# First attention of a two-layer decoder: the reciprocal root of the head norms moved from Newton steps on VectorE to one power on GpSimd

## Chip, cores and metric

The kernel runs on one core of one Trainium2 chip. The metric is the device time of one execution in microseconds (us). The engines are TensorE (PE; its weight loads are listed apart as PEld), VectorE (DVE), ScalarE (ACT), GpSimd (POOL) and SyncE (SP, which issues most of the transfers). Each engine takes its instructions strictly in order.

## What is computed

A decoder of two layers on x of 4 sequences of 256 tokens with 256 features, and a context of 4 x 256 tokens with 128 features. Each layer adds an attention, a state-space block (a scan over time with 16 states for each of 256 channels) and a feed-forward block to x. The change is in the first attention alone, whose queries, keys and values are normalised head by head:

```python
def _layernorm_unit(x, eps=1e-06):
    mu = jnp.mean(x, axis=-1, keepdims=True)
    xc = x - mu
    var = jnp.mean(xc * xc, axis=-1, keepdims=True)
    return xc * jax.lax.rsqrt(var + eps)
# 8 query heads, 2 key heads and 2 value heads of width 32; q and k are rotated (RoPE) first
q = _layernorm_unit(q) * 256.0
k = _layernorm_unit(k)
v = _layernorm_unit(v)
scores = einsum('bhqd,bhkd->bhqk', q, k) / sqrt(32) + mask   # causal, window of 64
scores = tanh(scores / 30.0) * 30.0
out = softmax(scores) @ v
```

## The kernel before

The first attention goes sequence by sequence (b = 0 to 3, 256 tokens each, in two chunks of 128 partitions). `head0(b)` (L347 to L408) makes the layer norm of x, transposes it, multiplies by the joint weight of q, k and v (L356), rotates q and k (L366, L372, L373), and subtracts the mean of each head (L380, L381). For both chunks together there are 24 heads (2 x 12), so one tile `rs` of 128 x 24 holds the mean squares: ScalarE squares (L385), VectorE sums (L388) and adds the epsilon (L389). `rsqrt_steps` (L100 to L112) then makes the reciprocal root on VectorE in 13 small instructions: a first guess from the bits of the number (L104) and three Newton steps of four instructions each (L108 to L111), one after the other on the same two tiles. VectorE scales the queries into `qn` (L396) and the values into `vn` (L399) by it, GpSimd the keys into `krep` (L403, twice). `tail0(b)` (L419 to L514) transposes `qn` and `krep` (L424, L429), forms the scores on TensorE (L449, L453), takes tanh and exp on ScalarE (L462, L470), weights the values (L476 to L487), divides by the sums (`divide`, L412 and L413), transposes (L497), projects (L506) and adds to x (L514).

Between these, in the same stage, runs the scan of the first state-space block, which doesn't depend on x: 64 states in all (2 halves of the batch x 2 halves of the channels x 16). One state takes an exponential on ScalarE (L215), a product `db` on GpSimd (L217), the scan on VectorE (L218), a product `hc` on VectorE (L220), and a sum of `hc` into y, in turns by a TensorE product with the identity (L235) and by an addition on GpSimd (L237). The row tiles `bt` and `ct` come by DMA from SP's queue (L209); `db`, `hc`, `bt` and `ct` have three buffers each, and the scanned tile `h` two. `mamba_front` (L150 to L200) prepares a half of the batch, with two softplus activations (L190). Behind the stage come the gate of the state-space block (L252 to L271), the first feed-forward (L606 to L638), and the second layer (from L641), in which `rsqrt` (L662 to L667) already takes a power on GpSimd (L666), as `ln_stats` does for the layer norms (L126).

The order in which the instructions of one engine stand is not that of the text: when the program is built, a list scheduler merges the two streams of work by its own estimate of when each instruction can start. A change of one line therefore moves its neighbours too. ScalarE loads a table before an activation of another kind than the last (the exponential of L215 and the softplus of L190 are such kinds), so the number of table loads depends on the order.

The constant tile `nhalf` (L94, L95) is 128 x 24 and holds -0.5.

Of the kernel before, what the change touches and what calls it, by code (L numbers as in the profile page):

```python
# [14 lines left out]
ALU = mybir.AluOpType  # L15
# [26 lines left out]
def decoder_kernel(  # L42
# [27 lines left out]
    nc = tc.nc  # L70
# [6 lines left out]
    def ps(pool):  # L77
        return pool.tile([P, 512], F32, tag="ps", name="ps")
# [15 lines left out]
    nhalf = cpool.tile([P, 24], F32, name="nhalf")  # L94
# [5 lines left out]
    def rsqrt_steps(v, n):  # L100

        r_ = small.tile([P, n], F32, tag=f"rs_r{n}", name="rs_r")
        t_ = small.tile([P, n], F32, tag=f"rs_t{n}", name="rs_t")
        nc.vector.tensor_scalar(  # L104
            r_.bitcast(I32), v.bitcast(I32), -0.5, float(0x5F3759DF), ALU.mult, ALU.add
        )
        for _ in range(3):
            nc.vector.tensor_mul(t_, r_, r_)  # L108
            nc.vector.tensor_mul(t_, t_, v)
            nc.vector.tensor_scalar(t_, t_, -0.5, 1.5, ALU.mult, ALU.add)  # L110
            nc.vector.tensor_mul(r_, r_, t_)  # L111
        return r_  # L112
# [17 lines left out]
    def ln_transposed(b, dst, pool):  # L130

        nb, rs = ln_stats([x[:, 2 * b + c, :] for c in range(2)])
        pt = ps(pool)
        for c in range(2):
            xn = work.tile([P, HID], F32, tag="xn", name="xn")
            nc.scalar.activation(
                xn, x[:, 2 * b + c, :], AF.Identity, bias=nb[:, c : c + 1], scale=rs[:, c : c + 1]
            )
            for f in range(2):
                nc.tensor.transpose(  # L140
                    pt[:, f * 256 + c * P : f * 256 + (c + 1) * P], xn[:, f * P : (f + 1) * P], ident
                )
        nc.scalar.copy(dst, pt.rearrange("p (f t) -> p f t", f=2))
# [175 lines left out]
    with ExitStack() as ph:  # L319
# [27 lines left out]
        def head0(b):  # L347
            xnT = work.tile([P, 2, S], F32, tag="xnT", name="xnT")
            ln_transposed(b, xnT, pa)

            r = ap.tile([P, 2, 12, 32], F32, tag="r", name="r")
            rr = ap.tile([P, 2, 10, 32], F32, tag="rr", name="rr")
            for c in range(2):
                pq = ps(pa)
                for f in range(2):
                    mm(  # L356
                        pq[:, 0:384],
                        lhsT=xnT[:, f, c * P : (c + 1) * P],
                        rhs=wqkv0[:, f, :],
                        start=(f == 0),  # L360
                        stop=(f == 1),
                    )
                cos = cst[:, C_COS0 + 32 * c : C_COS0 + 32 * c + 32]
                sin = cst[:, C_SIN0 + 32 * c : C_SIN0 + 32 * c + 32]
                q3 = pq[:, 0:320].rearrange("p (h d) -> p h d", d=32)
                nc.vector.tensor_mul(  # L366
                    rr[:, c].rearrange("p h (two d) -> p h two d", two=2),
                    pq[:, 0:320].rearrange("p (h two d) -> p h two d", two=2, d=16)[:, :, ::-1, :],
                    sin.rearrange("p (two d) -> p two d", two=2).unsqueeze(1).to_broadcast([P, 10, 2, 16]),
                )  # L370

                nc.vector.tensor_mul(q3, q3, cos.unsqueeze(1).to_broadcast([P, 10, 32]))  # L372
                nc.vector.tensor_add(r[:, c, 0:10, :], q3, rr[:, c])  # L373
                nc.scalar.copy(
                    r[:, c, 10:12, :], pq[:, 320:384].rearrange("p (h d) -> p h d", d=32)
                )

            rf = r.rearrange("p c h d -> p (c h) d")
            mean = small.tile([P, 24], F32, tag="a0_mean", name="a0_mean")
            nc.vector.tensor_reduce(mean, rf, AX.X, ALU.add)  # L380
            nc.vector.scalar_tensor_tensor(  # L381
                rf, mean.unsqueeze(2).to_broadcast([P, 24, 32]), -1.0 / 32, rf, ALU.mult, ALU.add
            )
            sq = ap.tile([P, 24, 32], F32, tag="sq", name="sq")
            nc.scalar.activation(sq, rf, AF.Square)  # L385
            rs = small.tile([P, 2, 12], F32, tag="a0_rs", name="a0_rs")
            rs24 = rs.rearrange("p c h -> p (c h)")
            nc.vector.tensor_reduce(rs24, sq, AX.X, ALU.add)  # L388
            nc.vector.tensor_scalar(rs24, rs24, 1.0 / 32, 1e-6, ALU.mult, ALU.add)  # L389
            rs = rsqrt_steps(rs24, 24).rearrange("p (c h) -> p c h", c=2)  # L390
            qn = ap.tile([P, 2, 8, 32], F32, tag="qn", name="qn")
            krep = ap.tile([P, 2, 2, 4, 32], F32, tag="krep", name="krep")

            vn = ap.tile([P, 2, 2, 33], F32, tag="vn", name="vn")
            nc.gpsimd.memset(vn[:, :, :, 32:33], 1.0)
            nc.vector.tensor_mul(  # L396
                qn, r[:, :, 0:8, :], rs[:, :, 0:8].unsqueeze(3).to_broadcast([P, 2, 8, 32])
            )
            nc.vector.tensor_mul(  # L399
                vn[:, :, :, 0:32], r[:, :, 10:12, :], rs[:, :, 10:12].unsqueeze(3).to_broadcast([P, 2, 2, 32])  # L400
            )
            for c in range(2):
                nc.gpsimd.tensor_mul(  # L403
                    krep[:, c],
                    r[:, c, 8:10, :].unsqueeze(2).to_broadcast([P, 2, 4, 32]),
                    rs[:, c, 8:10].unsqueeze(2).unsqueeze(3).to_broadcast([P, 2, 4, 32]),
                )
            return qn, krep, vn  # L408
# [117 lines left out]

        s0 = []
        parts = [head0(0), head0(1)]
        for b in range(B):
            states(2)  # L530
            if b + 2 < B:
                parts.append(head0(b + 2))
            tail0(b, *parts[b], states)
            if b == 0:
                first.append(mamba_scan(mamba_front(0, 1, pf), psd, psy))
            if b == 0:

                with tc.issue_after(loads[-1]):
                    nc.sync.dma_start(out=wqkv1, in_=wqkv1_in)
# [647 lines left out]
```

## Time and profile before

| what | value |
|---|---|
| three timed runs | 898.4, 910.52 and 914.03 us, median 910.52 us |
| the profiled execution's own time | 899.79 us |
| its span, first to last instruction | 898.0 us (1.79 us lie around it) |
| mean granted TensorE clock | 0.947 of full speed |
| PE, DVE, ACT, POOL busy | 806.3, 588.0, 474.5, 423.5 us |
| first attention, first `qn` to last addition to x | 33.1 to 188.5 us of the span |
| last state of the first scan | ends at 251.4 us |

The times in the prediction are positions in the profiled execution's span. A line of a group reads: source line, engine, operation, tile written <- tiles read, shapes, count, then the busy time of all in us and the mean of one in ns, then the idle time of the engine just before them and what ended most of it. A line of a timeline reads: start and length in us, engine, line, operation, tiles, shapes. In the table by stretches each engine has its busy time and, in brackets, its number of instructions, and then comes the granted clock of TensorE.

### The profile page before, as it was taken

Reading aid. Unit: us, or ns where it says so; the run is one execution under the profiler, and the core shown is the slowest. Engines: PE = TensorE matmul, PEld = TensorE weight load, DVE = VectorE, ACT = ScalarE, POOL = GpSimd, SP = SyncE. Lnnn points to the kernel's source line nnn. Section 1 sums busy time; section 2 is a strip of 40 time slices with the busy share of each in tenths; the row PEclk is TensorE's granted clock in tenths of the full one; section 3 lists DMA queues with packets and bytes.
Section 4 is the critical chain, followed back from the end, with each engine's and each line's share of the span. In section 5 each row is a group of like instructions: output and inputs, shape, how many; then the busy total and the mean of one; then the engine's idle time right before and its main releaser. Section 6 shows DMA issues by size and latency. Waiting matters only on the chain.

```text
span 898.0 us, 10284 instructions
## 1 busy us (share of the span) xinstructions
PE 806.3 (90%) x3074; PEld 501.4 (56%) x3074; DVE 588.0 (65%) x1106; ACT 474.5 (53%) x1182; POOL 423.5 (47%) x427
## 2 busy tenths in 40 slices
PE   4888999978989887889788978997999999999997
PEld 1445656523444444647555755665666656666665
DVE  4799988985855588797769686787057676212121
ACT  2767544587949556657857754776333433211111
POOL 5456676976645527766547471422257751000000
PEclk9999767978998999999899989997999999999999
DMA  5347564583512401101112010000147753445442
GB/s 162 117 133 252 174 187 157 186 275 100 198 64 68 143 1 36 59 33 39 36 36 72 23 47 1 24 3 24 27 152 226 231 152 104 148 149 162 156 144 82
DMA packets 60999, 98.36 MB, mean 110 GB/s; under 512 B 6336, under 2 KB 26704, under 8 KB 60688
## 3 DMA queue, kind: packets, MB, share of 16 engines
q1 hardware_dynamic: 59232, 95.77, 33.6%
q10 hardware_dynamic: 1712, 1.94, 0.7%
q8 instruction: 24, 0.39, 0.2%
q14 instruction: 31, 0.25, 0.1%
HBM read 96.24 MB, written 1.44 MB: 109 GB/s over the span
## 4 chain that ended last, share of the span: by engine, by line
PE 51%; DVE 20%; ACT 10%; issue 5%; POOL 4%; DMA 1%; DVEq 0%; POOLq 0%; SPq 0%; ACTq 0%
PE ps L974 13%; PE ps L988 12%; PE ps L842 5%; DVE h L218 4%; PE ps L673 3%; DVE hc L220 2%; PE ps L606 2%; PE ps L630 2%; PE ps L827 2%; DVE ps L700 2%; ACT sc L799 2%; DVE qs L693 2%; PE ps L780 1%; ACT L215 1%; PE ps L235 1%
## 5 line engine op out<-in xcount | busy, mean ns | idle before, releaser
L217 POOL TENSOR_TENSOR db<-bt,du 128x512 f32<-128x512 f32 x128 | 162.4, 1280 | 90.7 <-DVE h L218 76.3
L218 DVE TENSOR_TENSOR_SCAN h<-h,db 128x512 f32<-128x512 f32 x128 | 152.9, 1217 | 25.9 <-ACT h L215 25.7
L974 PE MATMUL ps<-moe_xnT,w 128*128 128x512 f32 x272 | 129.0, 597 | 0.0
L988 PE MATMUL ps<-w,hT 128*128 128x256 f32 x544 | 128.7, 380 | 0.0
L979 DVE SCALAR_TENSOR_TENSOR hT<-ps,gr 128x512 f32<-128x512 f32 x64 | 44.1, 689 | 127.0 <-PE ps L974 127.0
L988 PEld LDWEIGHTS ps<-w,hT 128*128 128x128 f32 x544 | 103.2, 191 | 40.2 <-issue 29.4
L215 ACT ACTIVATE h<-dt,negA 128x512 f32<-128x512 f32 x128 | 86.2, 689 | 56.3 <-DVE hc L220 55.7
L980 ACT ACTIVATE hT<-hT 128x512 f32<-128x512 f32 x68 | 42.8, 629 | 133.8 <-DVE hT L979 133.6
L673 PE MATMUL ps<-wqkv,xnT 128*128 128x512 f32 x192 | 93.2, 597 | 8.0 <-DVE rq L665 5.6
L220 DVE TENSOR_TENSOR hc<-h,ct 128x512 f32<-128x512 f32 x128 | 85.1, 680 | 4.0 <-DMA ct<-bc 2.5
L227 POOL TENSOR_TENSOR y<-y,hc 128x512 f32<-128x512 f32 x64 | 80.8, 1274 | 7.1 <-DVE hc L220 7.1
L666 POOL TENSOR_TENSOR rq<-rq,nhalf 128x8 f32<-128x8 f32 x20 | 33.0, 1648 | 88.2 <-DVE rq L665 88.0
L974 PEld LDWEIGHTS ps<-moe_xnT,w 128*128 128x128 f32 x272 | 51.7, 191 | 36.5 <-issue 33.2
L688 ACT ACTIVATE sq<-ps 128x128 f32<-128x128 f32 x160 | 42.4, 282 | 46.2 <-PE ps L673 46.2
L799 ACT ACTIVATE sc<-sc,nm 128x256 f32<-128x256 f32 (+1 forms) x128 | 56.7, 449 | 12.2 <-DVE nm L794 8.0
L804 POOL TENSOR_TENSOR sc<-sc,rsum 128x512 f32<-128x512 f32 (+1 forms) x32 | 46.3, 1468 | 35.2 <-DVE rsum L802 33.6
L842 PE MATMUL ps<-wo,oT 128*128 128x256 f32 x256 | 57.0, 381 | 0.4 <-ACT oT L835 0.4
L842 PEld LDWEIGHTS ps<-wo,oT 128*128 128x128 f32 x256 | 48.1, 190 | 9.2 <-ACT oT L835 2.6
L673 PEld LDWEIGHTS ps<-wqkv,xnT 128*128 128x128 f32 x192 | 32.9, 190 | 29.1 <-issue 17.9
L235 PE MATMUL ps<-hc,ident 128*128 128x512 f32 x64 | 40.6, 723 | 8.1 <-DVE hc L220 8.1
L707 PE MATMUL ps<-ident,qr 128*128 128x128 f32 x160 | 28.7, 297 | 19.2 <-DVE qr L701 17.3
L237 POOL TENSOR_TENSOR y<-y,hc 128x512 f32<-128x512 f32 x32 | 40.8, 1275 | 10.4 <-DVE hc L220 5.3
(201 smaller groups left out, 1447.3 us busy)
## 6 DMA issues: line engine op xcount, KB each, us to landing
bt<-bc SPq DMA_DIRECT2D x96, 256.0 KB, 3.6
ct<-bc SPq DMA_DIRECT2D x96, 256.0 KB, 3.7
w<-in_w_dram SPq DMA_DIRECT2D x64, 256.0 KB, 3.4
gr<-gt SPq DMA_DIRECT2D x64, 256.0 KB, 3.5
wqkv<-in_wqkv_dram SPq DMA_DIRECT2D x1, 3072.0 KB, 14.4
wo<-in_wo_dram SPq DMA_DIRECT2D x1, 2048.0 KB, 8.9
x<-in_x_dram SPq DMA_DIRECT2D x4, 256.0 KB, 5.6
w<-in_ws_dram SPq DMA_DIRECT2D x4, 256.0 KB, 3.4
```

Source lines behind the costliest of these rows:

```text
L215: nc.scalar.activation(h, dt[:, c, :], AF.Exp, scale=negA[:, a : a + 1])
L217: nc.gpsimd.tensor_mul(db, bt, du[:, c, :])
L218: nc.vector.tensor_tensor_scan(h, h, db, 0.0, ALU.mult, ALU.add)
L220: nc.vector.tensor_mul(hc, h, ct)
L227: nc.gpsimd.tensor_add(y[:, c, :], y[:, c, :], state(n, c, bt, ct))
L235: mm(yp, lhsT=ident, rhs=hc, start=(n == 0), stop=(n == 14))
L673: mm(pq, lhsT=xnT[:, f, c * P : (c + 1) * P], rhs=wqkv1[:, f, ch * 512 : (ch + 1) * 512], start=(f == 0), stop=(f == 1),)
L799: nc.scalar.activation(part, part, AF.Exp, bias=nm[:, qc, j : j + 1], accum_out=rsum[:, qc, j : j + 1])
L804: nc.gpsimd.tensor_mul(part, part, rsum[:, qc, :].unsqueeze(2).to_broadcast([P, 4, w]))
L842: mm(pout[:, c * 256 : (c + 1) * 256], lhsT=oTs[h // 4][:, h % 4, c * P : (c + 1) * P], rhs=wo1[:, 8 * gp + h, :], start=(h == 0), stop=(h ...
L974: mm(ph_, lhsT=w[:, f * P : (f + 1) * P], rhs=xnT[:, f, :], start=(f == 0), stop=(f == 1))
L988: mm(po[t // 2][:, (t % 2) * 256 : (t % 2 + 1) * 256], lhsT=h[:, t * P : (t + 1) * P], rhs=w[:, 256:512], start=start and t % 2 == 0, stop ...
```

## The change

One line of `head0` is replaced. The 13 VectorE instructions of `rsqrt_steps` are gone from it, and one GpSimd instruction takes the 128 x 24 tile to the power -0.5 in place; `qn`, `vn` and `krep` then read this tile. `rsqrt_steps` itself stays, since the second feed-forward uses it on another tile (L945).

```diff
             rs24 = rs.rearrange("p c h -> p (c h)")
             nc.vector.tensor_reduce(rs24, sq, AX.X, ALU.add)
             nc.vector.tensor_scalar(rs24, rs24, 1.0 / 32, 1e-6, ALU.mult, ALU.add)
-            rs = rsqrt_steps(rs24, 24).rearrange("p (c h) -> p c h", c=2)
+            nc.gpsimd.tensor_tensor(rs24, rs24, nhalf, ALU.pow)
             qn = ap.tile([P, 2, 8, 32], F32, tag="qn", name="qn")
```

In the program built from it, DVE has 52 instructions fewer and POOL 4 more. The order of all engines is the same up to the first `head0`, differs in the first attention and the first feed-forward, and is the same again from the last addition of the first scan (L239 of its second half) to the end. ACT has three more table loads in the part that differs: two for the softplus of L190 and one for the exponential of L215.

## The prediction

> **What bounds the kernel now.** I read the table by stretches first, to see which engine is full where the change sits, then the groups of the removed lines in 28 to 126 us, then VectorE's timeline around one of the removed blocks, and last the groups of the powers that GpSimd takes already. The stretches (length, busy time of PE, PEld, DVE, ACT, POOL, granted clock, DMA):
>
> ```profile
> 48.00:63.00 15.00, 13.48 (x66) 7.98 (x64) 14.99 (x31) 8.51 (x16) 8.82 (x8) 0.89 0.54 168
> 63.00:81.00 18.00, 16.27 (x76) 10.13 (x75) 17.79 (x33) 12.55 (x24) 11.44 (x12) 0.91 0.47 119
> ...
> 107.00:126.00 19.00, 16.81 (x78) 10.54 (x76) 17.72 (x33) 10.07 (x23) 15.61 (x15) 0.77 0.52 158
> 126.00:188.00 62.00, 59.46 (x266) 37.92 (x266) 51.18 (x71) 33.08 (x65) 50.02 (x45) 0.85 0.58 183
> ```
>
> DVE has no idle time from 48 to 81 us (14.99 of 15, 17.79 of 18): there it sets the pace, and three of the four blocks of Newton steps lie in stretches of this kind. From 126 us on PE is full (59.46 of 62) at a granted clock of 0.85, and DVE has some 11 us to spare. POOL goes from 59% to 82%. So a microsecond of DVE is worth something up to about 126 us and little behind.
>
> ```profile
> L110 DVE TENSOR_SCALAR rs_t<-rs_t 128x24 f32<-128x24 f32 x12 | 5.4, 448 | 0.1
> L108 DVE TENSOR_TENSOR rs_t<-rs_r 128x24 f32<-128x24 f32 x12 | 5.4, 447 | 0.2
> ...
> L111 DVE TENSOR_TENSOR rs_r<-rs_r,rs_t 128x24 f32<-128x24 f32 x12 | 3.4, 282 | 0.2
> ...
> L104 DVE TENSOR_SCALAR rs_r<-a_rs 128x24 int32<-128x24 int32 x4 | 3.3, 819 | 0.0
> ...
> L109 DVE TENSOR_TENSOR rs_t<-rs_t,a_rs 128x24 f32<-128x24 f32 x12 | 2.1, 173 | 0.1
> ```
>
> The same 128x24 work takes 173 ns in one line and 819 ns in another: the steps are stretched. The timeline of the second block shows where:
>
> ```profile
> 48.74 0.68 DVE L220 TENSOR_TENSOR hc<-h,ct 128x512 f32<-128x512 f32 x1
> 49.34 0.78 DVE L104 TENSOR_SCALAR rs_r<-a_rs 128x24 int32<-128x24 int32 x1
> 50.04 0.48 DVE L366 TENSOR_TENSOR rr<-ps,cst 128x320 f32<-128x320 f32 x1
> 50.44 0.17 DVE L108 TENSOR_TENSOR rs_t<-rs_r 128x24 f32<-128x24 f32 x1
> ...
> 52.14 1.00 DVE L110 TENSOR_SCALAR rs_t<-rs_t 128x24 f32<-128x24 f32 x1
> ...
> 62.81 0.92 DVE L396 TENSOR_TENSOR qn<-r,rs_r 128x512 f32<-128x512 f32 x1
> ```
>
> L104 lasts 0.78 us and ends when a POOL addition (48.82 to 50.09) ends; L110 lasts 1.00 and ends with a POOL product (51.83 to 53.10). And the block isn't one piece: scans and rotations stand between its steps, so DVE is never idle in it.
>
> ```profile
> L666 POOL TENSOR_TENSOR rq<-rq,nhalf 128x8 f32<-128x8 f32 x20 | 33.0, 1648 | 88.2 <-DVE rq L665 88.0
> ...
> L126 POOL TENSOR_TENSOR ln_rs<-ln_rs,nhalf 128x2 f32<-128x2 f32 x24 | 17.0, 713 | 1.7
> ```
>
> A power on POOL grows with the elements per partition: 6 more of them cost 1648 - 713 = 935 ns, 156 ns each.
>
> **What goes.** I count what each block takes of DVE: from its first step to `qn`, less the spacing of the other instructions in it. Block 0: 30.27 (end of L389) to 33.12, nothing between, 2.85 us. Block 1: 49.34 to 62.81 is 13.47, less 6 rotation steps at 0.40, 3 scans at 1.13, 3 `hc` at 0.60 and a reciprocal at 0.12 (7.73), leaves 5.74. Block 2: 70.70 to 80.09 is 9.39, less 3 scans, 2 `hc`, a reciprocal and a division (5.06), leaves 4.33. Block 3: 107.51 to 123.88 is 16.37, less 6 scans, 5 `hc`, three small ones and an idle 1.28 (11.63), leaves 4.74. Sum 17.66 us of DVE.
>
> **What comes.** The power on 24 elements isn't in the trace. From the two rows, a fixed 0.40 and 24 x 0.156 make 4.14 us; in proportion to the nearer row, 3 x 1.648 makes 4.94, and it can't take less than the 1.65 of a third of its size. I take 4.14, since two rows lie on it, and keep 4.94 for the range. Handing over costs little: L665 ends at 316.04, the power of L666 runs from 316.12 to 317.76, and DVE goes on at 317.80, 0.12 in all. Behind the power, in the order built from the change, `qn` stands on DVE directly after L389 (block 0), after L389 and one `hc` (blocks 1 and 2) or after L389 and one scan (block 3). So DVE, which takes its queue in order, stands idle, and the rotations and scans that used to fill the block are queued behind `qn`. On POOL the power has an addition of y (L237) ahead of it in blocks 1 and 2, which needs the `hc` just made, and a `db` in block 3. The wait on DVE:
> - Block 0: 4.14 + 0.12 = 4.26. Against 2.85: +1.41.
> - Blocks 1 and 2, on the old clock of block 1: `hc` is over at 49.34, L237 at 50.09, the power at 54.26, `qn` at 54.30: 4.96 idle. Against 5.74 and 4.33: -0.78 and +0.63.
> - Block 3: the `db` runs beside the scan, 4.26. Against 4.74: -0.48.
>
> Sum 18.44 of waiting for 17.66 of steps: +0.78 us. POOL gains 4 x 4.14 = 16.6 us, but while DVE waits no scan frees a `db` buffer either, and up to three finished `db` stand ready when the wait ends, so I cost the delay of the next `db` (power and two `krep`, 1.7 us) at nothing; if that stock is gone, it costs up to 1.7 per head.
>
> **Earlier `qn`.** After L389, `qn` came 14.0, 9.6 and 16.4 us later in blocks 1 to 3; now about 5. That looks like a gain, but TensorE transposed these `qn` at 74.2, 108.1 and 140.7, against `qn` finished at 63.7, 80.9 and 125.2: it wasn't waiting. I cost it at nothing. SP issues the same row loads in a new order; the three waits of `hc` for `ct` there make 2.5 us in all, and I leave them as they are.
>
> **New order elsewhere.** Three more table loads on ACT at 1.28 us. Two split the two softplus at 85 to 90 us by an exponential; ACT waited 1.73 us for TensorE between these (L190 at 89.11), so 2 x 1.28 - 1.73 leaves +0.8. The third lies near 196 us, where ACT waited 1.17 and 2.60, and is hidden. There the new order also has a gain: the addition of the gate of sequence 1 (L271 at 206.59) no longer stands behind the second `du` (L193 at 203.66, after 3.29 idle). Its ceiling is these 3.29 us, its floor nothing; I take half, -1.6.
>
> Sum: 0.78 + 0.8 - 1.6 = 0.0 us. On the profiled execution's own time that is 899.8. This execution lies 10.7 below the median; the four readings of the old kernel are two pairs, 898.4 and 899.8, and 910.5 and 914.0, so a median may fall in either, and I predict their mean, 905.7, rounded to 906.
>
> **Rules weighed.** The stretched steps first: the rows show 0.17 us alone and 0.78 to 1.00 against a POOL instruction. The Trainium skill ("SBUF — State Buffer", Who interferes with whom) says that VectorE and GpSimd share a port pair as an exclusive lock, which a two-input VectorE instruction or a two-port mode asks for, so the later one waits to the end; the trace agrees with its 1.00 beside 1.27. It would speak against a 4 us power on POOL, which would hold that pair; here DVE has nothing else to do in that time, so the sum is the same by it. The price second: the rows give 156 ns per element. The skill ("GPSIMD Engine Reference", Performance versus the Vector engine) gives about 2.6 cycles per element for a two-input add at 1.2 GHz; an estimate from that page would be 0.05 us for 24 elements above the fixed part, and the sum some 15 us faster. No row of a power agrees with it.
>
> **The rivals.**
> - *GpSimd becomes the bound (slower).* For it: POOL is 82% busy in 107 to 126. Against it: three `db` buffers, and PE is the fuller engine behind 126. Price: 4 x 0.80 for the power at its upper end, 4 x 1.27 for one more POOL instruction ahead of it, 4 x 1.7 for `krep` ahead of the next `db`, 3.0 for uncovered table loads: 3.2 + 5.1 + 6.8 + 3.0 = 18 us, 2.0%, 929 from the median and 930 from the upper pair. It decides as soon as the `db` stock is empty when the power ends, in more than two heads. Chance 0.17.
> - *The waits are filled (faster).* If TensorE and ScalarE, which go on while DVE waits, remove later waits of DVE (4.1 us for L506, 2.7 for L356, 12.9 for L215 in 28 to 260), half of the 17.66 comes through: -9, 897 from the mean. Against it: the later half is TensorE's. Chance 0.16; with the readings' lower pair it ends at 890. The whole 17.66 would be the ceiling, 1.9%.
> - *The clock.* TensorE had 0.77 to 0.87 of its clock from 107 to 253 us with 132 us of work; 0.05 more or less there is 132 x 0.05 / 0.85 = 7.8 us, in either direction: 898 or 914. Chance 0.12.
> - *No change that can be told*, as forecast: 0.55, on its own within 896 to 917 by the readings' scatter.
>
> **How the numbers follow.** The range runs from the lower pair less 9 (890) to the upper pair plus 12, two thirds of the slow rival (924). Within 2%, about what a measurement of this kernel can tell from no change, is 892 to 929 about the median 910.5. The forecast, the clock, half of the fast rival (0.08) and a quarter of the slow one (0.04) stay inside: 0.55 + 0.12 + 0.08 + 0.04, rounded to 0.78. Slower 0.13, faster 0.09.
>
> **What would show it.** The power at about 4.1 us, and DVE idle 4.3 to 5.0 before each `qn`, released by POOL; idle time of DVE in 28 to 126 up from 7 to about 25 us, its busy time down by about as much; the last addition to x (187.8) within 3 us. Wrong would be: a power far from 4.1; scans waiting for `db` after `krep`; that addition more than 8 us away.

## The result, and the profile after

The changed kernel took 913.7 us (median of 20 executions, 904.98 to 919.2), the kernel before 905.16 us beside it (20 executions, 898.4 to 915.4). The ratio is 1.0077, 95% interval 1.0048 to 1.0106: slower by 0.8%, or 7.0 us of some 906. The experiments' ratios below are turned into us in the same way; medians are over all executions and ratios leave disturbed ones out, so a ratio isn't always the quotient of the medians. No change was forecast; the change made the kernel slower by a small amount that these runs can tell from nothing.

The profiled execution of the changed kernel has a span of 913.6 us at a mean granted clock of 0.938, near its median. The one of before (898.0, 0.947) was among its fastest. Their positions therefore differ by more than the medians do, and I use them for mechanisms, and the medians for sizes.

The same stretches as before, in the changed kernel (length; busy time of PE, PEld, DVE, ACT, POOL with instructions in brackets; granted clock; DMA):

```profile
48.00:63.00 15.00, 11.45 (x59) 6.80 (x57) 10.17 (x14) 8.03 (x19) 12.12 (x9) 0.92 0.41 119
63.00:81.00 18.00, 16.28 (x71) 9.36 (x71) 12.89 (x20) 14.48 (x25) 13.13 (x9) 0.87 0.53 170
107.00:126.00 19.00, 12.86 (x61) 8.73 (x60) 10.41 (x15) 6.38 (x17) 12.68 (x9) 0.68 0.36 119
126.00:188.00 62.00, 56.54 (x256) 37.94 (x257) 46.80 (x68) 29.40 (x64) 48.65 (x44) 0.78 0.58 183
```

VectorE, which had no idle time from 48 to 81 us, is now busy for 68% and 72% of it (10.17 of 15, 12.89 of 18). Nothing took its place: TensorE does less in the first and third stretch too, and from 126 us on it is less full (56.54 for 59.46). The two groups that the change made or moved:

```profile
L390 POOL TENSOR_TENSOR a_rs<-a_rs,nhalf 128x24 f32<-128x24 f32 x4 | 16.7, 4176 | 4.9 <-DVE a_rs L389 4.9
...
L396 DVE TENSOR_TENSOR qn<-r,a_rs 128x512 f32<-128x512 f32 x4 | 2.8, 692 | 18.3 <-POOL a_rs L390 18.3
```

The power takes 4.18 us (4.14 was predicted), and VectorE waits 18.3 us for the four (18.44 was predicted). The timeline of VectorE in the second block has the pattern that the prediction drew, a gap where the steps, scans and rotations had been:

```profile
52.28 0.67 DVE L220 TENSOR_TENSOR hc<-h,ct 128x512 f32<-128x512 f32 x1
52.88 0.17 DVE L389 TENSOR_SCALAR a_rs<-a_rs 128x24 f32<-128x24 f32 x1
52.96 0.68 DVE L220 TENSOR_TENSOR hc<-h,ct 128x512 f32<-128x512 f32 x1
58.47 0.69 DVE L396 TENSOR_TENSOR qn<-r,a_rs 128x512 f32<-128x512 f32 x1 [4.83 <-POOL a_rs L390]
```

So both durations were right, and the end was still wrong. The chain of waits of the changed kernel says how much of this sets the end (start, length, engine, tile and line). All four powers lie on it, nearly whole, and make 16.7 us. From the first the chain goes on through the keys (`krep`) to TensorE, from the other three through VectorE:

```profile
30.93 4.19 POOL a_rs L390
35.19 1.13 POOL krep L403
36.36 0.33 PE ps L429
...
54.31 4.14 POOL a_rs L390
...
77.12 4.19 POOL a_rs L390
...
121.40 4.18 POOL a_rs L390
```

In the kernel before, the chain can be followed back to 83.9 us, which takes in the fourth block alone. There it passes through five of the 13 steps:

```profile
107.59 1.19 DVE rs_r L104
...
109.10 1.13 DVE rs_t L108
...
111.29 0.16 DVE rs_t L109
...
112.59 0.16 DVE rs_t L110
...
113.27 0.18 DVE rs_r L111
113.44 1.26 POOL db L217
...
115.09 4.80 DMA ct<-bc
```

The five steps are 2.82 us, and 2.32 of them are the two that were stretched. Then the chain leaves VectorE for a product on GpSimd and a row load; the other eight steps of the block, which ends at 123.88, don't lie on it. The prediction had counted 4.74 us for this block. That is the first sign of what was wrong, from one execution each: a wait for the power lies on the chain with its whole length, the steps only with a part of theirs.

VectorE's other waits from 28 to 126 us, before (waiting tile and line, releaser, us in total, times, longest):

```profile
DVE rr L366 <- PE ps L356: 2.7, 2, 1.7
DVE hc L220 <- DMA ct<-bc: 1.3, 1, 1.3
DVE a_rs L388 <- ACT sq L385: 1.0, 1, 1.0
```

and from 28 to 140 us after:

```profile
DVE qn L396 <- POOL a_rs L390: 18.3, 4, 4.8
DVE rr L366 <- PE ps L356: 5.4, 3, 4.6
DVE vn L399 <- PE ps L487: 4.4, 1, 4.4
DVE a_mean L380 <- ACT r L374: 2.6, 1, 2.6
```

Three small waits are new or longer beside the big one: the rotation for its product on TensorE (one of 4.6 us), `vn` for the reader of an older `vn` (two buffers), and the mean for ScalarE's copy. The ends of the stage, in the profiled executions (start of the last addition to x, of the gate addition of sequence 1, which is the second L271, and the span):

| kernel | last addition to x | second L271 | span | span less second L271 |
|---|---|---|---|---|
| before | 187.8 | 206.6 | 898.0 | 691.4 |
| changed | 207.6 | 221.4 | 913.6 | 692.2 |
| no power (first experiment) | 182.9 | 196.5 | 888.2 | 691.7 |
| power unread (ninth) | 195.0 | 209.0 | 902.3 | 693.3 |

The last column is the same within 2 us. Whatever differs has happened by the second L271, so the first attention and the scan beside it hold all of it.

### The profile page after: what moved, and what is told of

It is laid out like the page before. It is cut to its first block, busy times and chain, and to the rows that moved or that the text cites. A ratio compares the mean times of both kernels' runs of the same rounds, so it can differ in the third digit from the quotient of the medians.

```text
span 913.6 us, 10235 instructions
## 1 busy us (share of the span) xinstructions
PE 810.0 (89%) x3074; PEld 504.8 (55%) x3074; DVE 568.5 (62%) x1054; ACT 477.3 (52%) x1185; POOL 439.3 (48%) x431
## 4 chain that ended last, share of the span: by engine, by line
PE 58%; DVE 18%; ACT 10%; POOL 6%; issue 5%; DMA 2%; SPq 0%; DVEq 0%; ACTq 0%; POOLq 0%
PE ps L988 12%; PE ps L974 12%; PE ps L842 5%; DVE h L218 4%; PE ps L673 3%; PE ps L606 2%; PE ps L235 2%; PE ps L630 2%; PE ps L780 2%; POOL a_rs L390 2%; PE ps L827 2%; DVE hc L220 2%; DVE ps L700 2%; DVE qs L693 1%; ACT sc L799 1%
## 5 line engine op out<-in xcount | busy, mean ns | idle before, releaser
L215 ACT ACTIVATE h<-dt,negA 128x512 f32<-128x512 f32 x128 | 85.7, 689 | 64.8 <-DVE hc L220 64.3
```

The costliest lines, as they stand in the source:

```text
L215: nc.scalar.activation(h, dt[:, c, :], AF.Exp, scale=negA[:, a : a + 1])
```

## The experiments

The theories at the start. A: the waits of VectorE for the power lie on the path with their whole length, and the removed steps were worth less than the 17.66 us counted. B: GpSimd's time is the price, since a power holds back `db`, the y additions and `krep`. A third possibility is the new order (three table loads, single waits for a buffer).

**No power.** The line is deleted. The root is left out, so `qn`, `vn` and `krep` are scaled by the variance; every engine has the same order as in the changed kernel, but for one `krep` that stands two places earlier on GpSimd.

```diff
-            nc.gpsimd.tensor_tensor(rs24, rs24, nhalf, ALU.pow)
```

> This leaves the reciprocal root out: no Newton steps and no power, the mean square itself scales q, k and v. All engines keep the order of the changed kernel, so it shows what the four waits for the power cost there. Theory A (the waits lie on the path one to one, and the loss of 0.8% comes from the new order around them): about 18 us below the changed kernel, 11 below the kernel before, ratio 0.988. Rival B (the waits are mostly filled by other engines, and the loss is the power's hold on GpSimd and on the db tiles): 5 to 9 us below the changed kernel, ratio 0.998 to 1.002. Rival C (the order alone costs the time, the waits nothing): ratio 1.008, as the changed kernel.

Measured: 890.41 us, ratio 0.9853 (0.9814 to 0.9892), that is -13.3 us against before. The power and its waits cost 20.3 us between this kernel and the changed one. But taking out the steps, without any wait in their place, brought 13.3 and not 17.66. As busy time the count was right: over the whole program VectorE is busy for 588.0 us before and 570.3 us here, 17.7 less. So a microsecond off VectorE was worth less than a microsecond at the end.

Whether the next instruction inherits the stretching can be seen in the second block. VectorE:

```profile
48.86 0.16 DVE L389 TENSOR_SCALAR a_rs<-a_rs 128x24 f32<-128x24 f32 x1
48.94 0.68 DVE L220 TENSOR_TENSOR hc<-h,ct 128x512 f32<-128x512 f32 x1
49.54 1.29 DVE L395 TENSOR_TENSOR qn<-r,a_rs 128x512 f32<-128x512 f32 x1
50.76 0.70 DVE L398 TENSOR_TENSOR vn<-r,a_rs 128x128 f32<-128x128 f32 x1
```

and GpSimd in the same kernel:

```profile
49.02 1.27 POOL L237 TENSOR_TENSOR y<-y,hc 128x512 f32<-128x512 f32 x1
50.24 1.68 POOL L402 TENSOR_TENSOR krep<-r,a_rs 128x256 f32<-128x256 f32 x2
```

`qn` takes 1.29 us where the changed kernel's took 0.69, since it runs into the same GpSimd addition that had stretched the first step (L104) before. The mean of the four `qn` is 1.03 us here and 0.69 after the power, when GpSimd had just finished. In this block, with the step gone, the next instruction pays. The Trainium skill ("SBUF — State Buffer", Who interferes with whom) says why a two-input VectorE instruction can be held until a GpSimd instruction ends: they share a pair of ports, taken whole by whoever came first. This trace agrees: `qn` starts at 49.54 in the middle of the addition, and ends 0.54 us after it, a little under the 0.69 that a whole unstretched one takes. The stretching doesn't explain the missing 4.4 us, though: `qn` and `vn` together took 7.1 us before (3.7 and 3.4) and 6.5 here (4.1 and 2.4), and VectorE's busy time fell by all that was counted.

**A power on 8 of the 24 elements.** Only the first eight are raised (the others are left as variances, so the output is another one); the order is the same but for `vn` and `qn` of the first block.

```diff
-            nc.gpsimd.tensor_tensor(rs24, rs24, nhalf, ALU.pow)
+            nc.gpsimd.tensor_tensor(rs24[:, 0:8], rs24[:, 0:8], nhalf[:, 0:8], ALU.pow)
```

> The power is taken of 8 of the 24 columns only (the others stay mean squares), in the order of the changed kernel: the power should last 1.65 us instead of 4.18 and each wait fall by 2.5. Theory A: 10 us below the changed kernel, ratio 0.997. Rival B: 3 to 5 below, ratio 1.003. Rival C: no difference, 1.008.

Measured: 901.08 us, 0.9935 (0.9904 to 0.9966), -5.9 us. Its power and its wait:

```profile
L390 POOL TENSOR_TENSOR a_rs<-a_rs,nhalf 128x8 f32<-128x8 f32 x4 | 6.7, 1675 | 5.5 <-DVE a_rs L389 5.5
...
L396 DVE TENSOR_TENSOR qn<-r,a_rs 128x512 f32<-128x512 f32 x4 | 4.4, 1095 | 7.9 <-POOL a_rs L390 7.9
```

**The power twice.** A first power goes into a tile that nothing reads, and the real one follows on GpSimd.

```diff
+            spare_ = small.tile([P, 24], F32, tag="a0_sp", name="a0_sp")
+            nc.gpsimd.tensor_tensor(spare_, rs24, nhalf, ALU.pow)
             nc.gpsimd.tensor_tensor(rs24, rs24, nhalf, ALU.pow)
```

> The power is taken twice, once into a tile that nobody reads, in nearly the order of the changed kernel: 4 x 4.18 = 16.7 us more on GpSimd ahead of the power that is waited for. Theory A: 16.7 us above the changed kernel, ratio 1.026. Rival B: 6 to 10 above, ratio 1.015 to 1.019. Rival C: 1.008.

Measured: 926.01 us, 1.0249 (1.0197 to 1.0302), +22.5 us, with

```profile
L398 DVE TENSOR_TENSOR qn<-r,a_rs 128x512 f32<-128x512 f32 x4 | 2.8, 692 | 32.2 <-POOL a_rs L392 32.2
```

The four doses side by side:

| VectorE's wait for the power, us | against before, us |
|---|---|
| 0 (no power) | -13.3 |
| 7.9 (8 elements) | -5.9 |
| 18.3 (changed kernel) | +7.0 |
| 32.2 (twice) | +22.5 |

From 0 to 18.3 us of wait the time grows by 20.3, from there to 32.2 (13.9 more) by 15.5. That is 1.1 us for each. The wait plus what the power brings with it is paid whole, and there is no dose at which it is hidden. Theory A had said 0.988, 0.997 and 1.026 for the three kernels of this table that are new; the first and the last lie inside the measured intervals, the second 0.0004 above. This holds against the faster rival (the waits are filled), and a new order can't explain a slope among kernels whose order is one and the same, or nearly so (with two powers some neighbours have moved). GpSimd's time grows with the dose too, so these four don't separate it from the wait.

**Three buffers for `vn`.** It takes away the wait of `vn` for an older reader.

```diff
-            vn = ap.tile([P, 2, 2, 33], F32, tag="vn", name="vn")
+            vn = ap.tile([P, 2, 2, 33], F32, tag="vn", name="vn", bufs=3)
```

> The changed kernel with three buffers for vn instead of two. The wait of 4.4 us of the last vn for the products of an earlier sequence (L487) should go, and with it the order in the second half of the attention comes near to that of the kernel before. If theory A holds and the excess of 7 to 8 us comes from the order, most of it should go: ratio 1.000 to 1.003. If it comes from the power itself: 1.008 as the changed kernel.

Measured: 911.88 us, 1.0069 (1.0043 to 1.0095). That is 0.7 us from the changed kernel, inside the scatter, and the wait is gone from the waits of its profile. The 4.4 us wait was no cause.

**Newton steps that nobody reads.** In the changed kernel the steps come back in place of the power, and their result is dropped (the root is left out again).

```diff
-            nc.gpsimd.tensor_tensor(rs24, rs24, nhalf, ALU.pow)
+            rsqrt_steps(rs24, 24)
```

> No power; the 13 Newton steps run on VectorE as before, but nobody reads their result, the mean square scales q, k and v. So DVE has the work of the steps and qn waits for nothing. The run without root came out 13.3 us below the kernel before, where 17.7 us of steps had been counted. Theory D (the steps cost the DVE time that they take, 13 us of which is real, and a late qn costs nothing): as the kernel before, ratio 0.998 to 1.002. Rival E (a good part of the 13 us came from the earlier qn, not from the time of the steps): ratio 0.990 to 0.995.

Measured: 902.91 us, 0.9938 (0.9897 to 0.998), -5.6 us. Against the kernel without power the 52 steps cost 0.0085, or 7.7 us, with an interval of some 5 on each side. The number lies in rival E's range, and the interval just reaches theory D's 0.998. The rest of the 13.3, 5.6 us, came with `qn`, `vn` and `krep` being free of the steps, or with the order: it isn't that of either kernel (ScalarE has 1180 instructions here, 1185 without the power, 1182 before), and this run doesn't separate the two. The prediction had put an earlier `qn` at nothing.

**The scaling held back.** The power stays on GpSimd, but `qn`, `vn` and `krep` move to a function that is called before `tail0`, with an order that holds `qn` and `vn` until the 6th, 12th and 23rd scan in sequences 1 to 3, so that VectorE has other work while the power runs (`r` gets four buffers for it).

```diff
+        HOLD = [0, 5, 11, 22]
+
+        def scaled(b, r, rs):
...
+            with tc.issue_after(scanned[HOLD[b]]) if HOLD[b] else nullcontext():
+                nc.vector.tensor_mul(
+                    qn, r[:, :, 0:8, :], rs[:, :, 0:8].unsqueeze(3).to_broadcast([P, 2, 8, 32])
+                )
...
-            tail0(b, *parts[b], states)
+            tail0(b, *scaled(b, *parts[b]), states)
```

> The power stays on GpSimd, but the scaling of q and v is held on VectorE behind a scan that comes later (the 6th, 12th and 23rd state for sequences 1 to 3), so that scans of the other stream lie between L389 and qn; r has four buffers. Sequence 0 has nothing to put there and keeps its wait of 4.3 us. Theory A (the waits cost what they last, GpSimd's time nothing): 14 of the 18.3 us of waits go, 12 to 14 us below the changed kernel, ratio 0.992 to 0.995. Rival B (the hold of 4.2 us on GpSimd delays the db tiles and takes the place of the wait): ratio 1.002 to 1.008.

Measured: 911.94 us, 1.0038 (1.0001 to 1.0075), +3.4 us. VectorE's waits from 28 to 215 us:

```profile
DVE h L218 <- ACT h L215: 10.7, 7, 3.1
DVE rr L366 <- PE ps L356: 4.9, 1, 4.9
DVE x L520 <- PE ps L512: 4.8, 2, 3.1
DVE hc L220 <- DMA ct<-bc: 4.6, 4, 1.7
DVE qn L411 <- POOL a_rs L390: 4.3, 1, 4.3
DVE h L218 <- POOL db L217: 3.1, 2, 2.5
DVE hc L220 <- POOL y L237: 3.0, 1, 3.0
```

Three of the four waits for the power are gone, and the time hardly moved: 3.5 us below the changed kernel, with an uncertainty of 4. That is outside theory A's range and inside rival B's. New waits stand in their place, two of them for GpSimd (`db` 3.1, y 3.0). The longest of each ends soon after the fourth power, which runs from 108.31 to 112.48: 2.46 us for `db` until 114.96, 2.98 us for y until 119.76, with other work of GpSimd between. The last addition to x came at 194.1, 13.5 us ahead of the changed kernel's, but the second L271 at 218.0, only 3.4 ahead. So hiding the wait was not enough here. What took its place isn't separated: in sequences 1 to 3 `qn` starts 7 to 19 us after L389, where it was 5.6 in the changed kernel, and the order is a new one.

**Two Newton steps, and six.** The kernel before with another number of steps in this attention alone (`steps` becomes an argument of `rsqrt_steps`).

```diff
-            rs = rsqrt_steps(rs24, 24).rearrange("p (c h) -> p c h", c=2)
+            rs = rsqrt_steps(rs24, 24, 2).rearrange("p (c h) -> p c h", c=2)
```

> The kernel before with two Newton steps instead of three (16 VectorE instructions fewer in all), a candidate for a faster version. By the 13.3 us of 52 steps they are worth 0.26 us each, 4.1 us; the order also comes out with 13 table loads of 1.28 us fewer, since the states of the second scan are no longer put between the activations of the first feed-forward's second half. If the loads were hidden: ratio 0.995; if they count there: 16.6 us more, down to 0.977.

> The kernel before with six Newton steps instead of three: 48 VectorE instructions more. Theory D: 0.26 us each, 12.3 us, ratio 1.0136. If each cost its unstretched spacing of 0.216 us: 10.4, ratio 1.0115. If each cost what was counted with the stretching, 0.34 us: 16.3, ratio 1.018. If DVE is not the bound there: 1.000 to 1.004.

Measured: with two steps 902.08 us, 0.9972 (0.9933 to 1.0011), -2.5 us for 16 instructions fewer; with six 917.87 us, 1.01 (1.006 to 1.0139), +9.1 us for 48 more, 0.19 us each (0.11 to 0.26 by the interval). At that price 52 are worth 9.9 us. The interval leaves out 0.34 us a step, which is 17.66 over 52, and a price of nothing. The table loads that are missing with two steps were hidden, since 0.977 is far outside. By busy time a step costs more: VectorE has 583.2 us with two steps and 601.3 with six (588.0 before), so 0.30 and 0.28 us for each. The stretching moves among the lines. In the kernel with two steps:

```profile
L108 DVE TENSOR_TENSOR rs_t<-rs_r 128x24 f32<-128x24 f32 x8 | 4.7, 588 | 0.1
...
L110 DVE TENSOR_SCALAR rs_t<-rs_t 128x24 f32<-128x24 f32 x8 | 2.8, 346 | 0.1
```

With a third of the instances gone, the mean of L108 rose from 447 to 588 ns, and that of L110 fell from 448 to 346. All step lines together fell from 19.6 to 15.2 us, their mean rose from 0.38 to 0.42: a small part of the stretching passes to the steps that are left.

**The power unread.** The power runs on GpSimd into a tile that nothing reads, and `qn`, `vn` and `krep` take the variance (the root is left out). The order is that of the kernel without power, with the four powers added. It separates GpSimd's time from VectorE's wait.

```diff
-            nc.gpsimd.tensor_tensor(rs24, rs24, nhalf, ALU.pow)
+            spare_ = small.tile([P, 24], F32, tag="a0_sp", name="a0_sp")
+            nc.gpsimd.tensor_tensor(spare_, rs24, nhalf, ALU.pow)
```

> The power is taken as in the changed kernel, but into a tile that nothing reads: the root is left out of qn, vn and krep, and GpSimd is still held four times for 4.18 us. The instructions stand as in the run without the power (0.985 of before), with the four powers added on GpSimd alone. Theory (the wait of DVE for the power is the whole price, GpSimd's time is covered by the stock of db): 0.983 to 0.990, no wait of DVE for the power, end 692 us after the second gate addition (L271). Rival (GpSimd's 16.7 us themselves hold db, krep and the y additions back): at least half of the 20.3 us between that run and the changed kernel, 0.996 to 1.008, with DVE waiting for db or y after each power.

Measured: 897.42 us, 0.9892 (0.9837 to 0.9947), -9.8 us. GpSimd's time alone costs 3.5 us (0.9892 less 0.9853; an uncertainty of 6 from the two intervals), the reader's wait the other 16.8 of 20.3 (1.0077 less 0.9892; 6 as well). Theory A holds in size: 16.8 us for 18.3 us of wait. Theory B as the main cost is outside the interval, but it isn't empty. The profiled execution is the slowest of the six (904.1 us), so its positions are late. Its chain of waits goes through the first power by way of `krep`:

```profile
30.69 4.68 POOL a_sp L391
35.37 1.05 POOL krep L404
36.42 0.04 issue
36.46 0.48 PE ps L430
```

TensorE waits for the keys that stand on GpSimd behind the power, though they don't need it. Parts of the third and fourth power (0.37 and 1.84 us) lie on this chain too. The prediction had `krep` only as a cause of a late `db`.

**A shorter root on VectorE.** The kernel before, with two steps of three instructions in the first attention: eight per sequence in place of 13.

```diff
+        nc.vector.tensor_scalar(v, v, -0.5, None, ALU.mult)
+        for _ in range(2):
+            nc.vector.tensor_mul(t_, r_, r_)
+            nc.vector.tensor_mul(t_, t_, v)
+            nc.vector.scalar_tensor_tensor(r_, t_, 1.5, r_, ALU.add, ALU.mult)
```

> Before with a shorter root in the first attention alone: the variance is scaled by -0.5 once, each step is two products and one fused (t + 1.5) * r, and two steps are made instead of three: 8 DVE instructions per sequence in place of 13. Theory (a small step costs about 0.19 us on DVE, as in the run with six steps, 48 of which cost 9.1 us): 20 fewer are worth about 3.8 us, 0.996, with the order free to add or take 4 us: 0.991 to 1.001. Rival (each step was worth the 0.34 us counted in the prediction, 17.66 us for 52): 6.8 us or more, 0.993 or less, and with the first qn 1 us sooner each time. If DVE's steps cost nothing in this stage: 1.000.

Measured: 894.62 us (890.61 to 897.1), 0.9854 (0.9799 to 0.9909), -13.2 us. It is faster than both kernels, and by more than the theory's 0.991; the number falls on the rival's side. But it isn't a price per step that does it. The kernel with two plain steps has only four VectorE instructions more in all, and stands at 0.9972. What goes along with the time is the granted clock: the median over the executions was 0.958 here, where the kernel before had 0.937 beside it; with two plain steps it was 0.951, beside 0.940. Its order differs from before too, so it doesn't tell which part of the gain the shorter root earned and which the order or the clock.

## Why the prediction was wrong, point by point

- **The price of the power and the waits: right.** 4.18 us (predicted 4.14) and 18.3 us (18.44). The four waits were 4.29, 4.83, 4.83 and 4.37, against 4.26, 4.96, 4.96 and 4.26.
- **"Sum 17.66 us of DVE", what goes: wrong, and this is the step that failed.** As VectorE's busy time it was right (17.7). But it credited every microsecond of it, stretching included, as a gain at the end. Measured: 13.3 us (9.8 to 16.9) for the whole removal with no wait in its place, earlier `qn` and new order included; 7.7 us for steps that nobody reads; 9.9 us by the price of the added steps. With the two other terms (+0.8 and -1.6) the prediction's credit was 18.5 us, 5.2 more than measured. The rate of exchange, new orders included, came out below one in four comparisons: 13.3 us of time for 17.7 of busy time, 7.7 for 17.4 (steps unread against no power), 9.1 for 13.3 (six steps), 2.5 for 4.8 (two steps); the shorter root alone is out of line, with 13.2 for 7.0. Where the rest goes is shown in part: in the one block where the chain of before can be read, the steps hold 2.82 us of it, not 4.74, and without the power VectorE has a new wait of 4.2 us, of `vn` for TensorE (L486). But the wait of `vn` in the changed kernel cost nothing, and how much of the rest each of these is, no run shows.
- **The wait as a cost: nearly right.** 18.44 was charged in full, and 16.8 was paid, with an uncertainty of 6. With GpSimd's time the power cost 20.3 us, while the steps that it replaced had cost 13.3: that difference is the 7.0 us.
- **The delay of GpSimd's other work at nothing: mis-sized.** 3.5 us, though its uncertainty reaches nothing; the part that a chain shows is `krep`, in the first block above all. The kernel that held the scaling back speaks for a larger price, and the two aren't reconciled. The slower rival (18 us, GpSimd the bound) had the right sign for a part of its terms, but its mechanism, an empty stock of `db`, doesn't show: no line of VectorE's waits in the changed kernel up to 140 us names `db`.
- **Earlier `qn` at nothing: doubtful.** 5.6 of the 13.3 us (1.8 to 9.3) are left when the steps run unread. The order is new there too, so this isn't shown to be the earlier `qn`.
- **The sum.** Predicted -18.5 + 0 + 18.4 = 0.0. Measured -13.3 + 3.5 + 16.8 = +7.0.
- **The gate of sequence 1: right in sign, larger.** From the last addition to x to the second L271 it is 18.8 us before and 13.9 after, 4.9 less, where 1.6 were taken and 3.3 called the ceiling. Both positions are of one execution each, and whether the second `du` is the reason wasn't tested. The table loads: the part that differs has them as predicted; their +0.8 wasn't tested by itself.
- **The signs named beforehand.** The power and the waits came as said. VectorE's idle time from 28 to 126 us is 30.9 us, where about 25 was said (6.8 before). The last addition to x is 19.8 us later, far over the 8 us that were to show the prediction wrong; some 7 of it is that the two profiled spans lie 15.6 us apart and the medians 8.5.
- **The clock as a rival.** It named 914 for 0.05 less of the clock from 107 to 253 us. In the profiled execution the clock is 0.09 less from 107 to 126 us and 0.07 less from 126 to 188. That 913.7 was measured doesn't show this rival right, since the waits account for it as well.
- **What stays open.** How much of each difference comes by way of the granted clock. Over 58 executions of the kernel before, time and mean clock go together (correlation -0.86), at 7.3 us per 0.01. The medians of the clock are 0.942 before and 0.938 after, so about 3 of the 7.0 us can lie there. The kernel without power had 0.952 (0.942 before), which is enough for 7 of its 13.3 us; the one with the power unread 0.951 and the shorter root 0.958 (0.937 before), enough for all of their 9.8 and 13.2 us. Whether a wait lowers the clock (by bunching TensorE's work) or a lower clock only goes along, no run here separates. A power on VectorE wasn't tried.

The profiled executions show where the clock enters. Up to the second L271 TensorE has nearly the same work in all four kernels (704 or 705 matmuls):

| kernel | second L271 | TensorE busy | TensorE idle | granted clock |
|---|---|---|---|---|
| before | 206.6 | 174.3 | 32.3 | 0.87 |
| changed | 221.4 | 176.0 | 45.4 | 0.84 |
| no power | 196.5 | 163.1 | 33.4 | 0.90 |
| power unread | 209.0 | 173.2 | 35.8 | 0.84 |

From the power unread to the changed kernel (12.4 us) TensorE's idle time grows by 9.6 and its busy time by 2.7: the reader's wait shows mainly as idle time of TensorE, not as a lower clock. From before to no power it is the other way: the 10.1 us are all in shorter matmul time (11.1 less), and the idle time doesn't fall. So the gain from taking the steps out may have come by way of the clock, and the same holds for most of the price of GpSimd's time (10.1 of 12.5 us here). It is one execution of each kernel.

## What to carry to other kernels

Work taken from a full engine can be worth less than its busy time: here 0.44 to 0.75 of it in four comparisons out of five (in the fifth, the shorter root, the time fell by more). A wait in an in-order queue was worth nearly its whole length (16.8 us for 18.3), so an operation given to another engine must be needed late, and everything queued behind it there must be needed late too. To see which, run the operation there once with nobody reading it, and once not at all; the two differences are the price of the other engine's time and of the wait. Read the granted clock beside both.

## What the runs showed of the hardware

The power's price on GpSimd is close to linear: 0.71 us for 2 elements per partition, 1.65 to 1.68 for 8, 4.18 for 24. That is 156 to 158 ns per element. The Trainium skill ("GPSIMD Engine Reference", Performance versus the Vector engine) gives about 2.6 cycles per element for a two-input addition; no run here shows a power at that price. Where `qn` ran on VectorE beside the start of the power (in the kernel with the power unread), all four took 4.62 to 4.68 us and not 4.18: the stretching goes both ways.

The clock of TensorE fell early in some kernels. From 34 to 48 us it was granted 1.00 in the kernel before and only 0.76 in the changed one; the line of the kernel before and then that of the changed one:

```profile
34.00:48.00 14.00, 11.45 (x48) 6.00 (x48) 11.95 (x16) 11.41 (x20) 7.89 (x10) 1.00 0.63 208
```

```profile
34.00:48.00 14.00, 12.32 (x41) 5.99 (x40) 7.94 (x14) 7.99 (x12) 7.61 (x9) 0.76 0.50 156
```

TensorE is busy longer there (12.32 for 11.45) with fewer instructions (41 for 48), and the wait of 4.6 us for L356 falls into it. With three buffers for `vn` the same stage, with the same power, was granted 1.00 up to 56 us. With six Newton steps and no power on GpSimd it was granted 0.72 from 34 to 40 us. So this early fall isn't the power's own, though a single profile shows it as if it were. Each kernel was profiled once, so it isn't shown whether the fall belongs to a kernel's order or to the single execution.
